# Softmax inverses taken through DRAM as 16 to a partition, and 21 weight-sum items placed in the first attention

## The chip, the cores and the metric

The kernel runs on one core of a Trainium2 chip. The metric is the device time of one execution in microseconds (us). Everything is computed in fp32.

## What is computed

Two layers, cut to what matters here:

```python
# layer 0: attention over the 1024 positions of each of 4 images, 1024 channels, 16 heads of 64
qkv = x @ w_qkv.T + b_qkv
q, k = rmsnorm(rope(q)), rmsnorm(rope(k))          # over all 1024 channels
attn = softmax(q @ k.T * 64 ** -0.5)
out = rmsnorm((attn @ v) @ w_proj.T) + x
# layer 1: 1x1 conv (1024 to 256), 3x3 conv (256 to 256), 1x1 conv (256 to 1024),
# each with batch norm over the 4 images; relu after the first two; then
x = relu(x + softplus(residual_scale) * out)
```

## The kernel before

**Stages.** The images go one after the other (`for b in range(B)`): the Q, K and V projections, attention, the output projection (called y). Then come the first 1x1 convolution, the 3x3 convolution and the last 1x1 convolution. Channels lie on the 128 partitions, in 8 tiles of 128 (NT); the 1024 positions of an image are the free axis, in two halves of 512 (NCH).

**Fast products.** The large products are done by a Strassen-Winograd scheme, one level in the first Q and K projections (`project`), two levels elsewhere (`project2`). It needs sums of weight blocks (S1 to S4) and sums of activations. Weight sums are made once and kept in DRAM for later images: the outer sums in `wd`, the inner ones in `wd2`. The function `operands` (L223) loads four blocks, makes four sums on VectorE (L231 to L234) for the product at hand and stores them to `wd` (L237). The other sums are "items": `prepare` (L382, sums L387 to L390, stores L392) and `prepare_blocks` (L395, sums L404 to L407, stores L409). An item is four loads of 256 KB, four VectorE operations and four stores of 256 KB. There are seven items for each of the four weights (WQ, WK, WV, WP), and four block items for WV and for WP.

**Who sets the order.** The order on every compute engine is written by hand; SyncE's (SP) order is set by a scheduler. Each queue runs in order, and an instruction that waits holds all that is behind it. In projections a pace is kept: `product_done` is called after each product (a product of the one-level scheme is one unit of pace, one of the two-level scheme half a unit), `after(n, step)` puts a step n units later, and `waiting` holds steps that are taken when there is room. `weight_parts(parts, first, step, lag, alloc)` starts an item's loads on GpSimd's queue (POOL) at `first + i * step` and makes its sums `lag` later.

**Attention.** `attention` (L740) runs once for each half of the queries (c), and within it over the 8 pairs of heads (hp). One such step is called a unit here, 16 to an image. A unit has 16 score products (L757) into three score banks, 8 exponentials on ScalarE (L764), 7 additions on VectorE that sum the exponentials into `den` (L766, L768), 16 steps of the product with V (L774), and a copy of the result into `q_all` (L779). After each odd unit, ones-products (`dn`, L800) turn the denominators of two units into a bank in which each 32 partitions hold one head's 512 denominators. At the start of the next unit `inverses` (L805) takes VectorE's reciprocal of the whole bank (L806) and sends one row per head to `dens` in DRAM, for a later check, and eight pieces from partition to partition into the tile `inv` (L814). At the end of the next odd unit `mean_of_v` multiplies the results by it (L737) and GpSimd adds a bias (L738).

At the end of a unit one step of `waiting` is taken (the last of K's rotation), and an `extra` step: the sums of the oldest item, and then at once the loads of another into the ring of eight weight buffers (`wring`); two items are in flight. In the first attention 15 items are done in this way, in the last one the sums of the 3x3 filters.

**The other places.** Of the remaining items, eight lie in the first Q projection (four blocks and four of WV), five in the first K projection (three of WV, two of WQ), three of WQ in the first V projection, two of WK in the first output projection, two in the second image's Q projection and one in its K projection. At the end of the image loop `conv1_first(1, ...)` (L899) does the first two products of the 1x1 convolution, and then `conv1_sums` (L873) makes the sums of its weights.

Of the kernel before, what the change touches and what calls it, by code (L numbers as in the profile page):

```python
# [18 lines left out]
P = 128  # L19
# [5 lines left out]
CH = 512  # L25
# [60 lines left out]
def program(ctx, tc, x, wblk, w2, w3, vecs, cos, sin, out, bad):  # L86
# [66 lines left out]
    with tc.tile_pool(name=f"st{u}", bufs=2) as st, ExitStack() as s:  # L153
# [70 lines left out]
        def operands(base, g, name):  # L224


            at = base // NT * NG + g
            a11, a12 = (block(base, g, ih, f"{name}_1{ih}") for ih in range(2))
            a21, a22 = (block(base, g + NG, ih, f"{name}_2{ih}") for ih in range(2))
            s1 = chunk(f"w_{name}_s1")  # L230
            nc.vector.tensor_tensor(s1, a21, a22, ALU.add)  # L231
            nc.vector.tensor_tensor(a21, a11, a21, ALU.subtract)
            nc.vector.tensor_tensor(a11, s1, a11, ALU.subtract)
            nc.vector.tensor_tensor(a12, a12, a11, ALU.subtract)  # L234
            spend(4 * TT)
            for o, t in enumerate((a11, s1, a21, a12)):
                nc.gpsimd.dma_start(wd[at, o], flat(t))  # L237
            return [a11, s1, a21, a12, a22]
# [501 lines left out]
        def attention(b, c, q_all, k_all, v, probs_, late, ready, extra, slow):  # L740
# [4 lines left out]
            for hp in range(NHP):  # L745
# [6 lines left out]
                for t in range(N // P):  # L752
                    p = probs_[:, t]
                    sc = bank("sc", f"sc_{n}_{t}")
                    for j in range(2):
                        d = slice(j * HD, (j + 1) * HD)
                        nc.tensor.matmul(  # L757
                            sc[:, j], k_all[d, hp, t * P : (t + 1) * P], q_all[d, hp, at],
                            start=True, stop=bad is not None,
                        )  # L760
                    if bad is None:
                        for j in range(2):
                            nc.tensor.matmul(sc[:, j], ones[0:1, :], rows[j], start=False, stop=True)
                    nc.scalar.activation(p, sc, AF.Exp)  # L764
                    if t == 1:
                        nc.vector.tensor_tensor(d_, probs[0], p, ALU.add)  # L766
                    elif t > 1:
                        nc.vector.tensor_tensor(d_, d_, p, ALU.add)  # L768
                    probs.append(p)
# [11 lines left out]
                if hp % 2 == 1:  # L781
                    for r in ready:
                        mean_of_v(q_all, *r)
                    ready.clear()
                if slow:
                    slow.pop(0)()

                left = (NCH - c) * NHP - hp - 1
                turn = bool(waiting)
                if turn:  # L790
                    next_waiting()
                if extra and (not turn or len(extra) >= left):
                    extra.pop(0)()
# [9 lines left out]

        def inverses(b, c, hp, n, dn, ready):
            r = temp(f"rec_{n}")  # L805
            nc.vector.reciprocal(r, dn)  # L806
            k = 2 * ((b * NCH + c) * NHP + hp - 1)
            if bad is not None:
                nc.sync.dma_start(dens[k : k + 4, :], r[::QH, :])
            w = big_temp(f"inv_{n}")  # L810
            for i in range(2):
                for j in range(4):
                    q = slice((2 * i + j // 2) * QH, (2 * i + j // 2 + 1) * QH)
                    nc.sync.dma_start(w[j * QH : (j + 1) * QH, half[i]], r[q, :])  # L814
                ready.append((c, hp - 1 + i, w[:, half[i]]))
# [249 lines left out]
        for b in range(B):  # L1065
# [12 lines left out]
            elif b == 1:  # L1078
                weight_parts([parts_of[WK][k] for k in (4, 5)], 8.5, 3.5, 3.5, pieces_of(room[:, : NT // 2, :]))
# [9 lines left out]
            elif b == 1:  # L1089
                weight_parts([parts_of[WK][6]], 11, 0, 3.5, pieces_of(room[:, : NT // 2, :]))  # L1090
# [3 lines left out]
            if b == 0:  # L1094
                two2 = [None, None, in_place(xs[b], ts[b], room, True)]

                t3 = pieces_of(xs[b][:, :NH, half[1]], 1)
                for k, at, free in ((6, 11, pieces_of(ts[b][1], 1)), (2, 14.5, t3), (3, 18.5, pieces_of(ts[b][1], 1))):
                    weight_parts([parts_of[WQ][k]], at, 0, 3.5, free)
# [6 lines left out]
            if b == 0:  # L1106
                todo = blocks_of(WP) + [parts_of[WP][k] for k in (0, 1, 6, 2, 3, 4, 5)]
                todo += [parts_of[WQ][k] for k in (4, 5)] + [parts_of[WK][k] for k in (0, 1)]
            made = []

            def extra_step():
                if len(made) == 2 or not todo:
                    made.pop(0)()
                if todo:
                    made.append(todo.pop(0)(pieces, nc.sync))

            extra = [extra_step] * len(todo)
            for _ in range(min(2, len(todo))):
                extra_step()
            if b == B - 1:  # L1120
                extra = filters()
            late, ready = [], []
# [9 lines left out]
            for c in range(NCH):  # L1132
                attention(b, c, q_all, k_all, v, probs_, late, ready, extra, slow)
# [45 lines left out]
            if b == 0:  # L1179
                weight_parts([parts_of[WK][k] for k in (2, 3)], 6, 7, 4, pieces_of(room[:, 3 * NT // 4 :, :]))  # L1180
# [14 lines left out]
        read_back(0)  # L1195
        conv1_first(1, back[1], w)
        ss = conv1_sums(w)
# [355 lines left out]
```

## Time and profile before

| | |
|---|---|
| Runs | 2701.3 us median of three, 2698.25 to 2702.26 |
| Profiled execution | 2699.65 us, of which its span is 2697.9 us |
| Instructions | 32539 |
| TensorE, VectorE, ScalarE, GpSimd busy | 98%, 81%, 41%, 17% |
| One attention unit on TensorE | 7.07 us of scores, 7.02 us of products with V; 1.0 us of dn after every second |
| Reciprocal of a 128x512 bank (L806) | 32 times, 3.354 us each |
| An addition of the denominators (L768) | 384 times, 1.225 us each |

The span is the stretch from the first to the last instruction of one profiled execution. A timeline lists the instructions of an engine in order of time, equal neighbours merged: its start, its duration, the line, the operation, the tile written and those read, how many, and in brackets how long the engine had been idle and which engine or transfer ended that. The busy times by stretch give, for each stretch of time, how long each engine was busy. Where TensorE is the engine without idle time, the idle time of the others costs nothing.

### The profile page before, as it was taken

The page shows a single profiled execution, that of the slowest core. Times are in us where ns is not written, and L with a number is a line of the kernel's source. Part 1 is how long each engine was busy: PE and PEld are TensorE (multiplying, and loading weights), DVE is VectorE, ACT ScalarE, POOL GpSimd, SP SyncE. Part 2 cuts the span into 40 slices and gives each one's busy share as a digit, 9 for nine tenths or more (in the row PEclk, how much of TensorE's full clock was granted, in tenths as well). Part 3 has the DMA queues.
Part 4 walks back from the last instruction along what each step waited for, and adds up shares of the span by engine and source line. Part 5 has one row for each costly group of instructions (what it writes and reads, how often), then busy time and mean ns, then how long its engine had stood idle before and what let it go on. Part 6 is the DMA issues. An engine that isn't in the chain of part 4 may idle for free. (4 is left out here: it accounts for less than half of the span.)

```text
span 2697.9 us, 32539 instructions
## 1 busy us (share of the span) xinstructions
PE 2656.7 (98%) x11386; PEld 1652.7 (61%) x11386; DVE 2194.8 (81%) x2529; ACT 1097.2 (41%) x1523; POOL 461.2 (17%) x568
## 2 busy tenths in 40 slices
PE   9999999999999999999999999999999999999997
PEld 4448433488888333688886333888884335846843
DVE  5577899998887977888878877887888878777987
ACT  2222455523342555333343555233525654312266
POOL 2562222222011211100111211100111211010000
PEclk9999999999999999999999999999999999999999
DMA  7897755587677341456765420665783323583165
GB/s 273 310 310 228 227 157 162 167 268 246 197 206 215 64 90 32 149 152 220 189 184 153 82 60 17 209 205 174 189 234 87 63 49 114 169 256 117 63 227 211
DMA packets 244811, 453.52 MB, mean 168 GB/s; under 512 B 28256, under 2 KB 117136, under 8 KB 244640
## 3 DMA queue, kind: packets, MB, share of 16 engines
q1 hardware_dynamic: 200112, 302.33, 35.7%
q0 software_dynamic: 44528, 149.02, 20.9%
q8 instruction: 93, 1.52, 0.2%
q14 instruction: 78, 0.64, 0.1%
HBM read 316.71 MB, written 96.78 MB: 153 GB/s over the span
## 5 line engine op out<-in xcount | busy, mean ns | idle before, releaser
L768 DVE TENSOR_TENSOR den<-den,p 128x1024 f32<-128x1024 f32 x384 | 470.5, 1225 | 40.7 <-DVE den L768 0.9
L764 ACT ACTIVATE p<-sc 128x1024 f32<-128x1024 f32 x512 | 476.3, 1043 | 54.9 <-PE sc L757 54.7
L757 PE MATMUL sc<-q,k 64*128 64x512 f32 x2048 | 457.7, 596 | 0.0
L757 PEld LDWEIGHTS sc<-q,k 64*128 64x128 f32 x2048 | 189.9, 186 | 265.5 <-issue 121.2
L774 PE MATMUL cx<-p,to 128*64 128x512 f32 x1536 | 340.2, 595 | 0.0
L774 PEld LDWEIGHTS cx<-p,to 128*64 128x64 f32 x1536 | 106.0, 137 | 228.2 <-issue 228.2
L738 POOL TENSOR_SCALAR q<-q,vec 128x512 f32<-128x512 f32 x64 | 123.7, 1939 | 561.7 <-DVE q L737 561.7
L458 PE MATMUL p_y<-q,w_y 128*128 128x256 f32 x928 | 210.1, 380 | 1.1 <-DMA w_y<-wdf 1.1
L453 PE MATMUL p_v<-w_v,x 128*128 128x256 f32 x928 | 210.1, 380 | 0.6 <-DVE x L424 0.6
L458 PEld LDWEIGHTS p_y<-q,w_y 128*128 128x128 f32 x928 | 175.9, 190 | 28.5 <-issue 4.8
L453 PEld LDWEIGHTS p_v<-w_v,x 128*128 128x128 f32 x928 | 176.5, 190 | 25.8 <-DVE x L424 1.3
L779 ACT COPY q<-cx 128x512 f32<-128x512 f32 x64 | 37.6, 587 | 356.9 <-PE cx L774 356.9
L458 PE MATMUL p_k<-to,w_k 128*128 128x256 f32 x672 | 153.1, 381 | 4.7 <-ACT to L547 4.7
L458 PE MATMUL p_q<-to,w_q 128*128 128x256 f32 x672 | 152.5, 380 | 0.7 <-ACT q L512 0.6
L458 PEld LDWEIGHTS p_k<-to,w_k 128*128 128x128 f32 x672 | 126.7, 190 | 25.8 <-ACT to L547 7.1
L458 PEld LDWEIGHTS p_q<-to,w_q 128*128 128x128 f32 x672 | 127.2, 190 | 20.2 <-ACT q L512 1.9
L766 DVE TENSOR_TENSOR den<-p 128x1024 f32<-128x1024 f32 x64 | 76.5, 1195 | 76.2 <-ACT p L764 76.2
L806 DVE RECIPROCAL rec<-dn 128x512 f32<-128x512 f32 x32 | 107.3, 3352 | 20.6 <-PE dn L800 20.6
L774 PE MATMUL cx<-p,rq 128*64 128x512 f32 x512 | 113.4, 595 | 0.0
L1457 PE MATMUL c<-h,w 128*128 128x512 f32 x256 | 110.3, 592 | 0.9 <-ACT h L1359 0.9
L700 POOL DMA_DIRECT2D k<-ks x64 | 55.6, 1011 | 276.5 <-ACT p L764 110.9
L453 PE MATMUL p_v<-w_v,t 128*128 128x256 f32 x384 | 91.6, 384 | 3.6 <-DMA w_v<-in_wblk_dram 3.6
(479 smaller groups left out, 4212.8 us busy)
## 6 DMA issues: line engine op xcount, KB each, us to landing
w_v<-wd2f SPq DMA_DIRECT2D x112, 256.0 KB
w_y<-wd2f SPq DMA_DIRECT2D x112, 256.0 KB
w_q<-wd2f SPq DMA_DIRECT2D x84, 256.0 KB
w_k<-wd2f SPq DMA_DIRECT2D x84, 256.0 KB
x<-in_x_dram SPq DMA_DIRECT2D x64, 256.0 KB
q<-qs POOLq DMA_DIRECT2D x64, 256.0 KB, 5.6
k<-ks POOLq DMA_DIRECT2D x64, 256.0 KB, 4.6
inv<-rec SPq DMA_DIRECT2D x256, 64.0 KB
```

The costliest lines, as they stand in the source:

```text
L453: nc.tensor.matmul(o[:, q].rearrange("p (g f) -> p g f", g=2), r[:, i, q * P : (q + 1) * P], wt[:, :, i, :], skip_group_check=True, **at,)
L458: nc.tensor.matmul(o[:, q], wt[:, q, i, :], r[:, i, :], skip_group_check=True, **at)
L700: nc.gpsimd.dma_start(dst[i::2, f, :], other[1 - i :: 2, :], accum_op=ALU.add)
L738: nc.gpsimd.tensor_scalar(cx, cx, col("bv", hp), None, ALU.add)
L757: nc.tensor.matmul(sc[:, j], k_all[d, hp, t * P : (t + 1) * P], q_all[d, hp, at], start=True, stop=bad is not None,)
L764: nc.scalar.activation(p, sc, AF.Exp)
L766: nc.vector.tensor_tensor(d_, probs[0], p, ALU.add)
L768: nc.vector.tensor_tensor(d_, d_, p, ALU.add)
L774: nc.tensor.matmul(o[j * HD : (j + 1) * HD, :], v[:, t, h0 : h0 + HD], probs[t][:, j], start=(t == 0), stop=(t == N // P - 1),)
L779: nc.scalar.copy(q_all[:, hp, at], o)
L806: nc.vector.reciprocal(r, dn)
L1457: nc.tensor.matmul(os[i], w3t[k][f // NH][:, f % NH, :], h2[b, k][:, half[c]], start=(k == 0), stop=(k == NPT - 1),)
```

## The change

Five edits:

- `operands` stores its four sums from ScalarE's queue instead of GpSimd's, one product later.
- In attention the denominators of four heads are copied by ScalarE, written to DRAM as rows, and read back as 16 to a partition; at the end of the next (even) unit VectorE inverts this 128x16 tile in place, it is written back to the same rows, and eight broadcasts from DRAM fill `inv`. The last pair of units of an image keeps the old way.
- 21 items instead of 15 are done in the first attention: six come from other places (one of WQ from the first V projection, five of WK from the first output projection and the second image's Q and K projections), and the two WQ items that stay in the first V projection are timed anew. They are spread evenly over 15 units, so that units 2, 4, 7, 9, 12 and 14 (counted from 0) make two. The last attention's filter sums are spread by the same rule.
- The loads of an item begin after the fourth score block of a unit (`t == 3`) rather than at the end of the unit before.
- `conv1_sums` is called ahead of `conv1_first`.

```diff
@@ -233,8 +233,12 @@
             nc.vector.tensor_tensor(a11, s1, a11, ALU.subtract)
             nc.vector.tensor_tensor(a12, a12, a11, ALU.subtract)
             spend(4 * TT)
-            for o, t in enumerate((a11, s1, a21, a12)):
-                nc.gpsimd.dma_start(wd[at, o], flat(t))
+
+            def keep():
+                for o, t in enumerate((a11, s1, a21, a12)):
+                    nc.scalar.dma_start(wd[at, o], flat(t))
+
+            after(1, keep)
             return [a11, s1, a21, a12, a22]
 
 
@@ -737,7 +741,7 @@
             nc.vector.tensor_tensor(cx, cx, w, ALU.mult)
             nc.gpsimd.tensor_scalar(cx, cx, col("bv", hp), None, ALU.add)
 
-        def attention(b, c, q_all, k_all, v, probs_, late, ready, extra, slow):
+        def attention(b, c, q_all, k_all, v, probs_, late, ready, extra, slow, steps_in_all, load_parts):
 
 
             at = half[c]
@@ -762,6 +766,8 @@
                         for j in range(2):
                             nc.tensor.matmul(sc[:, j], ones[0:1, :], rows[j], start=False, stop=True)
                     nc.scalar.activation(p, sc, AF.Exp)
+                    if t == 3:
+                        load_parts()
                     if t == 1:
                         nc.vector.tensor_tensor(d_, probs[0], p, ALU.add)
                     elif t > 1:
@@ -782,14 +788,15 @@
                     for r in ready:
                         mean_of_v(q_all, *r)
                     ready.clear()
+                if half_done:
+                    half_done.pop(0)()
                 if slow:
                     slow.pop(0)()
 
-                left = (NCH - c) * NHP - hp - 1
-                turn = bool(waiting)
-                if turn:
+                if waiting:
                     next_waiting()
-                if extra and (not turn or len(extra) >= left):
+                slots = NCH * NHP - 1
+                for _ in range(len(extra) - -(-steps_in_all * max(slots - 1 - c * NHP - hp, 0) // slots)):
                     extra.pop(0)()
                 if hp % 2 == 0:
                     continue
@@ -801,17 +808,36 @@
                 sums_ = []
                 late.append(lambda *a, n=n, hp=hp, dn=dn: inverses(b, c, hp, n, dn, ready))
 
+        half_done = []
+
         def inverses(b, c, hp, n, dn, ready):
+
+
             r = temp(f"rec_{n}")
-            nc.vector.reciprocal(r, dn)
             k = 2 * ((b * NCH + c) * NHP + hp - 1)
-            if bad is not None:
+            if (c, hp) == (NCH - 1, NHP - 1):
+                nc.vector.reciprocal(r, dn)
                 nc.sync.dma_start(dens[k : k + 4, :], r[::QH, :])
+                spread(c, hp, n, ready, [r[q * QH : (q + 1) * QH, :] for q in range(4)])
+                return
+            nc.scalar.copy(r, dn)
+            nc.sync.dma_start(dens[k : k + 4, :], r[::QH, :])
+            few = st.tile([P, 4 * CH // P], F32, tag="few", name=f"few_{n}")
+            rows = dens[k : k + 4, :].rearrange("r (a t) -> (r a) t", t=4 * CH // P)
+            nc.sync.dma_start(few, rows)
+
+            def invert():
+                nc.vector.reciprocal(few, few)
+                nc.sync.dma_start(rows, few)
+                spread(c, hp, n, ready, [dens[k + q, :].partition_broadcast(QH) for q in range(4)])
+
+            half_done.append(invert)
+
+        def spread(c, hp, n, ready, rows):
             w = big_temp(f"inv_{n}")
             for i in range(2):
                 for j in range(4):
-                    q = slice((2 * i + j // 2) * QH, (2 * i + j // 2 + 1) * QH)
-                    nc.sync.dma_start(w[j * QH : (j + 1) * QH, half[i]], r[q, :])
+                    nc.sync.dma_start(w[j * QH : (j + 1) * QH, half[i]], rows[2 * i + j // 2])
                 ready.append((c, hp - 1 + i, w[:, half[i]]))
 
         def o_norm(b, total, ys):
@@ -1075,8 +1101,6 @@
                 unused = kp.tile([P, NT, N], F32, tag="k", name="unused")
                 parts = blocks_of(WV) + [parts_of[WV][k] for k in (0, 1, 6, 2)]
                 weight_parts(parts, 8, 2.4, 4, pieces_of(unused))
-            elif b == 1:
-                weight_parts([parts_of[WK][k] for k in (4, 5)], 8.5, 3.5, 3.5, pieces_of(room[:, : NT // 2, :]))
             tq = qk_proj(b, WQ, xs[b], ts[b], "bq", q_all, "q", w1 if b == 0 else None, two, True)
             rope(b, q_all, tq, eps_q, HD / C, None, "q", b == 0)
             k_all = kp.tile([P, NT, N], F32, tag="k", name=f"k_{b}")
@@ -1086,17 +1110,13 @@
             if b == 0:
                 parts = [parts_of[WV][k] for k in (3, 4, 5)] + [parts_of[WQ][k] for k in (0, 1)]
                 weight_parts(parts, 2, 4.5, 4, pieces_of(room))
-            elif b == 1:
-                weight_parts([parts_of[WK][6]], 11, 0, 3.5, pieces_of(room[:, : NT // 2, :]))
             tk = qk_proj(b, WK, xs[b], ts[b], "bk", k_all, "k", None, two)
             rope(b, k_all, tk, eps_rms, 1.0 / C, (wqk_other, wqk), "k")
             v = room
             if b == 0:
                 two2 = [None, None, in_place(xs[b], ts[b], room, True)]
 
-                t3 = pieces_of(xs[b][:, :NH, half[1]], 1)
-                for k, at, free in ((6, 11, pieces_of(ts[b][1], 1)), (2, 14.5, t3), (3, 18.5, pieces_of(ts[b][1], 1))):
-                    weight_parts([parts_of[WQ][k]], at, 0, 3.5, free)
+                weight_parts([parts_of[WQ][k] for k in (6, 2)], 11.5, 6.5, 4, pieces_of(ts[b][1], 1))
             project2(b, 1, WV, *two2[2], b == 0, v, True, "v", lambda c: None)
 
             rest(leave=4 if b > 0 else 2)
@@ -1105,21 +1125,19 @@
             todo = []
             if b == 0:
                 todo = blocks_of(WP) + [parts_of[WP][k] for k in (0, 1, 6, 2, 3, 4, 5)]
-                todo += [parts_of[WQ][k] for k in (4, 5)] + [parts_of[WK][k] for k in (0, 1)]
+                todo += [parts_of[WQ][k] for k in (3, 4, 5)] + [parts_of[WK][k] for k in (0, 1, 6, 2, 3, 4, 5)]
             made = []
 
-            def extra_step():
-                if len(made) == 2 or not todo:
-                    made.pop(0)()
-                if todo:
+            def load_parts():
+
+                while todo and len(made) < 2:
                     made.append(todo.pop(0)(pieces, nc.sync))
 
-            extra = [extra_step] * len(todo)
-            for _ in range(min(2, len(todo))):
-                extra_step()
+            extra = [lambda: made.pop(0)()] * len(todo)
+            load_parts()
             if b == B - 1:
                 extra = filters()
-            late, ready = [], []
+            late, ready, steps_in_all = [], [], len(extra)
 
             def add_residual(f, b=b - 1):
                 nc.gpsimd.dma_start(
@@ -1130,7 +1148,7 @@
             slow = [lambda: None] * 3 + [lambda f=f: add_residual(f) for f in range(NT)] if b > 0 else []
             probs_ = xp.tile([P, N // P, 2, CH], F32, tag="x", name=f"p_{b}")
             for c in range(NCH):
-                attention(b, c, q_all, k_all, v, probs_, late, ready, extra, slow)
+                attention(b, c, q_all, k_all, v, probs_, late, ready, extra, slow, steps_in_all, load_parts)
             psum_for("proj")
             room = v_room(f"to_{b}")
             tc_ = [
@@ -1176,8 +1194,6 @@
 
                 for i in range(0, NH, 2):
                     after(14 + 3 * i, lambda i=i: waiting.append((5 * TT, lambda: first_sums(i))))
-            if b == 0:
-                weight_parts([parts_of[WK][k] for k in (2, 3)], 6, 7, 4, pieces_of(room[:, 3 * NT // 4 :, :]))
             yt[b] = kp.tile([P, NT, N], F32, tag="k", name=f"y_{b}")
             two = (2, *in_place(q_all, tc_, yt[b], False), True)
             if b + 1 < B:
@@ -1193,8 +1209,8 @@
         read_back(2)
         back[0] = v_room("back")
         read_back(0)
+        ss = conv1_sums(w)
         conv1_first(1, back[1], w)
-        ss = conv1_sums(w)
         for i in range(0, NH, 2):
             t_sums(back[1], None, t2[i], i, range(3, 4))
         room1, sums2 = t1, t2
```

## The prediction

> **What bounds the kernel now.** I read the page's busy times first, then TensorE's timeline from end to end for its gaps, then the same stretches on VectorE (DVE), ScalarE (ACT), GpSimd (POOL) and SyncE's queue (SP), then the busy times by stretch. The first line of the page:
>
> ```profile
> PE 2656.7 (98%) x11386; PEld 1652.7 (61%) x11386; DVE 2194.8 (81%) x2529; ACT 1097.2 (41%) x1523; POOL 461.2 (17%) x568
> ```
>
> TensorE is idle for 2697.9 - 2656.7 = 41.2 us. Its timeline puts 5.75 of that ahead of the first matmul and 15.1 behind the last one (which ends at 2669.76 + 13.04 = 2682.8). About 20 us lie between, and no edit here changes the matmuls, so only these can be won. The larger gaps, from TensorE's timeline (start, us, then in brackets the idle time before it and who ended it):
>
> ```profile
> 168.23 3.70 PE L298 MATMUL pa_k<-t,w_k_2b 128*128 128x512 f32 x8 [0.94 <-DVE w_k_2b L233]
> 187.30 3.70 PE L298 MATMUL pa_k<-t,w_k_3b 128*128 128x512 f32 x8 [1.63 <-DVE w_k_3b L233]
> 276.81 3.40 PE L453 MATMUL p_v<-w_v,t 128*128 128x256 f32 x8 [3.65 <-DMA w_v<-in_wblk_dram]
> 280.01 2.21 PE L453 MATMUL p_v<-w_v,x 128*128 128x256 f32 x8
> 282.06 1.89 PE L453 MATMUL p_v<-w_v,t 128*128 128x256 f32 x8
> ...
> 563.53 1.97 PE L458 MATMUL p_y<-q,w_y 128*128 128x256 f32 x8 [1.10 <-DMA w_y<-wdf]
> 662.80 1.99 PE L458 MATMUL p_q<-t,w_q 128*128 128x256 f32 x8 [0.67 <-DMA w_q<-wdf]
> 749.35 1.99 PE L458 MATMUL p_k<-t,w_k 128*128 128x256 f32 x8 [0.56 <-DMA w_k<-wdf]
> 783.05 7.17 PE L458 MATMUL p_k<-to,w_k 128*128 128x256 f32 x32 [2.35 <-ACT to L547]
> 1359.42 7.17 PE L458 MATMUL p_k<-to,w_k 128*128 128x256 f32 x32 [0.81 <-ACT to L547]
> 2362.05 5.37 PE L894 MATMUL c<-t,c_S 128*128 128x512 f32 x8 [3.06 <-DVE c_S L878]
> 2367.26 3.60 PE L894 MATMUL c1s<-to,c_S 128*128 128x512 f32 x8
> ```
>
> Two gaps cost more than they show. After 3.65 us the next eight matmuls take 280.01 - 276.81 = 3.20 us from start to start and the next 2.05, against 1.73 elsewhere: 1.47 + 0.32 more, 5.44 in all. After 3.06 us they take 5.21 against 3.43: 1.78 more, 4.84 in all. After 2.35 us nothing is lost.
>
> The four attentions, by stretch (PE, PEld, DVE, ACT, POOL busy; clock; DMA share; GB/s):
>
> ```profile
> 295.96:530.69 234.73, 234.66 (x1089) 84.08 (x1088) 220.99 (x203) 129.83 (x145) 66.20 (x82) 1.00 0.54 164
> 879.00:1113.00 234.00, 234.00 (x1092) 84.50 (x1090) 186.19 (x150) 129.71 (x145) 40.97 (x36) 1.00 0.27 55
> ```
>
> TensorE has no gap there: the first attention, with DVE 94% busy, is 0.7 us longer than the second. A faster DVE in attention buys nothing. The question is where the moved work stops hurting, and whether the fuller first attention stays covered.
>
> **What the Trainium skill says.** "TensorE: Matmul & The Clock Gate", Part 1, says that an idle window of about 3.4 us, which is free-running, drops the array to half clock. This trace agrees: near half rate after 3.65 and 3.06 us, none after 2.35. "DMA: Bandwidth & Descriptors", section Issuing engines are not separate DMA queues, says that DMAs of ACT, SP and POOL share 16 engines and another issuer saves only issue time. So I expect ACT's stores to relieve POOL's queue, not the bandwidth. Anatomy of one DMA, same page, puts a small DMA at about 2 us, mostly completion; here the 4 KB inv_df write of L676 lands after 2.1 us.
>
> **The change, part by part.**
>
> *Sums of the last convolution's weights (conv1_sums) ahead of conv1_first.* DVE is idle from 2354.3 to 2359.1, waiting for TensorE's c1a (L910), and the four sums queue behind that. Moved ahead, they run in the idle time (4 x about 0.68 = 2.7 us) and are ready near 2357; TensorE wants them at 2358.99. Of their ring slots the last is freed when p_y ends at 2352. The gap and its clock loss go: 4.84. Next late is the sum of squares for ss_y: its DVE adds (L588) and one ACT square end about 0.5 us after TensorE would now arrive. Gain 4.3.
>
> *Third weight item in the first V projection goes to attention; the others start at 11.5 and 18.* Between 260 and 280 us the DMA share is 1.03 at 334 GB/s. The load that TensorE misses was issued at 266.3 and was needed at 273.2, among an item's load on POOL (258 to 261.5, landing 9.5 us after issue), another's stores (260.9 to 265.4) and a rope accumulation. The item of 258 goes away: 1 MB of loads and 1 MB of stores. What is left is one item's stores ahead and the next load behind. Between 0 and 5.44 gained; I take 4.0.
>
> *Operand stores of the first Q and K from POOL to ACT.* Each set takes POOL 4 x 0.54 us, 3.6 with its waits at 168.6. Behind it stand the item loads that DVE then waits for (5.37 us ahead of 182.32), and DVE's lateness makes the 0.94 and 1.63 gaps. On ACT the four issues (SP's take 0.36 each, so about 1.5 us) wait for the DVE sums; behind them ACT has squares and the copy of the A22 product. The next copy that TensorE needs is a product later (3.43 us) or more, so this is covered unless the sums come over 3 us late, when TensorE waits for them anyway. But the DMA share is 1.02 here and stays. 0 to 2.6 gained; I take 2.0.
>
> *Items out of the first output projection (two), second Q (two) and second K (one).* Each is 2.9 us of DVE, 1 MB in and 1 MB out, on POOL. Loads sit just ahead of the gaps: 547.8 before 563.53, 660.7 before 662.80, 741.9 before 749.35; the 783.05 gap is 0.81 in later images, which have no items. Winnable: 1.10 + 0.67 + 0.56 + (2.35 - 0.81) + a 0.63 gap at 621.38 behind a busy DVE = 4.5. I take 3.5.
>
> *Softmax inverses.* 28 of 32 reciprocals (3.354 us) go: 94 us of DVE, hidden, worth nothing by themselves. Added: an ACT copy (0.59, like L779's) behind dn while the first scores run (0.9 us), so covered; and a 128x16 reciprocal, which the trace doesn't show: the 128x256 row is 1.75 and 128x512 3.35, so a line through them gives 0.24 us; bounds 0.1 and 1. The chain is now denominators to DRAM, back as 128x16, inverted at the end of the next unit, to DRAM, eight broadcasts back. On SP the eight take 5 to 6 us, with 2 us each side: about 10 us from a reciprocal to its multiplication L737, which DVE reaches 12 to 15 us later.
>
> *21 items instead of 15 in the first attention.* Let E be the start of an even unit; a unit is 14.09 us. From DVE's timeline, denominators start at the earliest 3.15 us into a unit and end at 12.36:
>
> ```profile
> 402.10 1.22 DVE L766 TENSOR_TENSOR den<-p 128x1024 f32<-128x1024 f32 x1 [0.22 <-ACT p L764]
> 403.43 7.88 DVE L768 TENSOR_TENSOR den<-den,p 128x1024 f32<-128x1024 f32 x6
> 411.22 1.29 DVE L737 TENSOR_TENSOR q<-q,inv 128x512 f32<-128x512 f32 x2
> ```
>
> The spread rule makes two items in units 2, 4, 7, 9, 12 and 14. For an even one: 12.36 + 0.3 + 2 x 2.9 = E + 18.5, the odd unit's denominators take 9.2 more, E + 27.7; TensorE needs them for dn at E + 28.2. It fits by 0.5 us. The small read must land by E + 12.4. On SP it stands behind weight loads that wait for POOL's stores of the unit before, which stand behind POOL's two 2.1 us bias adds: stores from E + 3.1, first landing (2.8) near E + 6.2, read landing about E + 11 to 12. So near nothing, with little room: between 0.7 gained (the first attention's excess) and some 10 lost. I take 1.5 lost. In the later attentions DVE has 48 of 234 us free: nothing.
>
> Sum: 4.3 + 4.0 + 2.0 + 3.5 - 1.5 = 12.3. The profiled execution took 2699.65 (span 2697.9, 1.75 around it), so 2687.35. The median of the runs shown is 2701.3, 1.65 above it: 2689.0.
>
> **The rivals.** (A) Bandwidth, not POOL's order, makes the K and V gaps, and they stay (for it: shares of 1.02 and 1.03; against: 2 MB leave the V stretch). 4.3 + 3.5 - 1.5 = 6.3 gained: 2695.0. (B) The small reads land 3 us later than I think, the double units' reciprocals wait, and dn waits 2.5 us in four pairs: 13.8 - 10 = 3.8 gained, 2697.5. For it: SP's order, and the 0.5 us of room; against: landings of 2.3 to 4.6 us in this stretch. (C) Slower: the broadcasts from DRAM land after L737 wants them, and DVE stands with everything behind it. In the first attention a pair has 3.6 us of slack there, so TensorE loses what exceeds that, seven times; in the others the slack is near 9.9 us. At 7 us late: 7 x 3.4 = 24 lost, 13.8 - 24 = 10 worse, 2711. It decides from 6.3 us late. For it: three dependent DMAs where one was, all on SP's queue; against: 2.1 us for a small write, 0.6 per broadcast issue.
>
> **How the numbers follow.** My forecast 0.52, A 0.18, B 0.17, C 0.13. About 0.2% (5.4 us) is what measurement can tell from no change. Faster by more: forecast and A, 0.70; within: B, 0.17; slower: C, 0.13. The best ends give 4.8 + 5.4 + 2.6 + 4.5 + 0.7 = 18, 2683.3; with the runs' spread, 2682. Upward the range takes in A and B, to 2699, and leaves out C.
>
> **What would show it.** The gap at c_S gone; no wait for w_v near 273; gaps at w_k_2b and w_k_3b under 0.5; 783's gap at 0.8; the first attention within 234.0 to 236.5. Waits of DVE before the 128x16 reciprocal or L737 with gaps at dn would make it B or C; unchanged K and V gaps, A.

## The result, and the profile after

The changed kernel takes 2690.1 us (median of 7 runs, 2688.6 to 2694.9), the kernel before 2701.3 (median of 7 runs, 2698.3 to 2707.1). The ratio is 0.9959, with a 95% interval of 0.9948 to 0.9971: about 11 us faster, against 12.3 in the forecast (2689.0). The profiled execution of the changed kernel took 2691.15 us, its span 2689.1, so the two profiled executions are only 8.5 us apart: before's was 1.65 under its median, this one is 1.0 over its own. What follows from single profiles is read against these 8.5.

The first line of the page after:

```profile
PE 2655.3 (99%) x11386; PEld 1650.9 (61%) x11386; DVE 2109.6 (78%) x2529; ACT 1112.6 (41%) x1551; POOL 426.8 (16%) x512
```

VectorE has lost 85 us of work and TensorE 1.4. The gain is not the 85; it is idle time of TensorE that went, 41.2 us before and 2689.1 - 2655.3 = 33.8 now, and clock losses. TensorE's timeline after, at the places that were shown of before:

```profile
9.27 15.14 PE L302 MATMUL pa_q<-x,w_q 128*128 128x512 f32 x30 [1.54 <-DMA x<-in_x_dram]
...
189.39 5.40 PE L302 MATMUL pa_k<-t,w_k_3b 128*128 128x512 f32 x8 [2.54 <-DVE w_k_3b L233]
...
256.97 1.97 PE L457 MATMUL p_v<-w_v,t 128*128 128x256 f32 x8 [0.73 <-DMA w_v<-wdf]
...
777.50 7.17 PE L462 MATMUL p_k<-to,w_k 128*128 128x256 f32 x32 [0.81 <-ACT to L551]
...
2354.97 3.60 PE L920 MATMUL c<-t,c_S 128*128 128x512 f32 x8
2358.41 3.60 PE L920 MATMUL c1s<-to,c_S 128*128 128x512 f32 x8
2362.04 0.64 PE L670 MATMUL ss_y<-sqy,ones 128*32 128x256 f32 x8
```

The gap ahead of c_S is gone and so is its clock loss; the 3.65 ahead of w_v has become 0.73 at another place; 2.35 has become 0.81. But the gap ahead of w_k_3b, the last of K0's four sets of operands, has grown, with a clock loss of its own, and the first line is new: a wait for x at the start of the kernel.

To see what every edit does, I take the time at which TensorE starts each stage, and from it each stage's length. This table carries most of what follows; each number is from one profile (us). "Q0" is the first image's Q projection, "C1" the first 1x1 convolution.

| Stage | before | after | difference |
|---|---|---|---|
| Q0 | 98.81 | 101.28 | +2.47 |
| K0 | 100.01 | 101.40 | +1.39 |
| V0 | 91.40 | 86.76 | -4.64 |
| first attention | 234.73 | 234.54 | -0.19 |
| Y0, Q1, K1 | 263.34 | 258.82 | -4.52 |
| C1 | 105.33 | 100.44 | -4.89 |
| all the others, and the start | | | +1.65 |
| end of the last matmul | 2682.80 | 2674.07 | -8.73 |

How far one profile carries can be read from two kernels below whose code is that of the kernel before up to the end of V0 (sums first alone, inverses alone). There K0 is 101.44 and 101.99 us, against 100.01 in the table, and V0 88.83 and 89.15, against 91.40. So in these two stages a difference of up to 2.6 us can come without any edit. Y0, Q1 and K1 together repeat better: 263.3 to 264.5 us in the four kernels with the old items there, 258.1 to 260.2 in the nine without.

The attentions, by stretch (the columns are as in the prediction):

```profile
295.12:529.66 234.54, 234.47 (x1089) 84.41 (x1088) 214.46 (x226) 133.80 (x152) 77.47 (x106) 1.00 0.68 218
873.95:1107.39 233.44, 233.44 (x1090) 84.28 (x1089) 163.77 (x149) 133.79 (x152) 42.27 (x36) 1.00 0.28 55
```

With six items more, the first attention has less VectorE work than before (214.5 against 221.0 us) and is no longer.

### The profile page after: what moved, and what is told of

Its sections match the earlier page's. It is cut to its first block, busy times and chain, and to the rows that moved or that the text cites. A ratio compares the mean times of both kernels' runs of the same rounds, so it can differ in the third digit from the quotient of the medians.

```text
span 2689.1 us, 32699 instructions
## 1 busy us (share of the span) xinstructions
PE 2655.3 (99%) x11386; PEld 1650.9 (61%) x11386; DVE 2109.6 (78%) x2529; ACT 1112.6 (41%) x1551; POOL 426.8 (16%) x512
## 5 line engine op out<-in xcount | busy, mean ns | idle before, releaser
L462 PE MATMUL p_y<-to,w_y 128*128 128x256 f32 x384 | 90.4, 380 | 0.9 <-DMA w_y<-wdf 0.8
```

What stands on the lines that cost most here:

```text
L462: nc.tensor.matmul(o[:, q], wt[:, q, i, :], r[:, i, :], skip_group_check=True, **at)
```

## The experiments

All kernels here compute the whole reference. The stage lengths are again from one profile of each.

**One part alone: sums first, ACT stores, inverses.** Three kernels, each the kernel before with one edit.

```diff
+        ss = conv1_sums(w)
         conv1_first(1, back[1], w)
-        ss = conv1_sums(w)
```

> The kernel before with one edit: conv1_sums ahead of conv1_first. My theory: the gap of 3.06 us at c_S and its clock loss of 1.78 us go, some 0 to 0.5 us comes back at ss_y: 4.3 to 4.9 us faster than before, and every stage up to the last output projection as in the kernel before. Rival (the gap is only moved to the next wait, for back or for ss_y): under 1.5 us faster, with a new gap within 20 us behind the old one.

Measured: 2695.2 us against 2701.4, ratio 0.9979 (0.9972 to 0.9986). C1 goes from 105.33 to 100.44, the same as in the changed kernel. That the stages ahead would be as before did not hold: K0 is 1.4 us longer and V0 2.6 shorter, with nothing edited there. In the changed kernel the sums stand well ahead of their use, and the squares for ss_y end at 2358.91 + 3.07 = 2361.98, just as TensorE comes for them at 2362.04:

```profile
2349.74 0.69 DVE L903 TENSOR_TENSOR c_S<-w_c_last,w_c_last 128x512 f32<-128x512 f32 x1
...
2358.91 3.07 DVE L592 TENSOR_TENSOR sqy<-sqy,sq_y 128x512 f32<-128x512 f32 x4
```

So the whole 4.89 is won; the 0.5 that I had taken off for ss_y isn't lost.

```diff
-            for o, t in enumerate((a11, s1, a21, a12)):
-                nc.gpsimd.dma_start(wd[at, o], flat(t))
+            def keep():
+                for o, t in enumerate((a11, s1, a21, a12)):
+                    nc.scalar.dma_start(wd[at, o], flat(t))
+
+            after(1, keep)
```

> The kernel before with one edit: the operand stores of the first Q and K on ScalarE's queue, one product later. If POOL's queue made the gaps in K (as I took it in the prediction): 2 us faster, both gaps of K under 0.5 us. If bandwidth makes them (rival A): within 1 us of before, or some us slower; one gap of K stays, its wait ended by a load of the weights[...].

Measured: 2705.0 us, ratio 1.0010 (1.0003 to 1.0018). The edit costs some 3 us where I had forecast a gain of 2. TensorE's timeline of this kernel:

```profile
9.67 16.13 PE L302 MATMUL pa_q<-x,w_q 128*128 128x512 f32 x30 [1.89 <-DMA x<-in_x_dram]
...
189.56 3.70 PE L302 MATMUL pa_k<-t,w_k_3b 128*128 128x512 f32 x8 [1.44 <-DVE w_k_3b L233]
```

The gap at w_k_3b stays (1.63 before), and the new wait for x is there: Q0 is 102.30, 3.5 us longer than before. This gave a new theory, which the trace of POOL's queue suggests. In the kernel before, POOL stands for 30 us with the first store, and the item loads stand behind it:

```profile
32.41 0.57 POOL L237 DMA_DIRECT2D wdf<-w_q_0b  x1 [30.44 <-DVE w_q_0b L233]
...
34.56 2.14 POOL L401 DMA_DIRECT2D unused<-in_wblk_dram  x4
```

In the changed kernel nothing holds POOL, and eight item loads (2 MB, of which the first sums are stored only at 52.45 us) are issued at once:

```profile
1.95 3.74 POOL L405 DMA_DIRECT2D unused<-in_wblk_dram  x7
7.36 0.54 POOL L405 DMA_DIRECT2D unused<-in_wblk_dram  x1 [1.67 <-DMA vec<-in_vecs_dram]
```

They meet the loads of x and w_q. SyncE's queue, first before and then after, shows these taking up to twice as long to issue:

```profile
3.06 1.60 SPq L221 DMA_DIRECT2D w_q<-in_wblk_dram  x3
4.70 2.87 SPq L210 DMA_DIRECT2D x<-in_x_dram  x4
```

```profile
3.07 3.15 SPq L221 DMA_DIRECT2D w_q<-in_wblk_dram  x3
6.26 4.28 SPq L210 DMA_DIRECT2D x<-in_x_dram  x4
```

The activation sums on VectorE that start at 17.14 us before start at 23.84 after, waiting for x, and everything behind them is late. The runs on the stores below put this to the test.

The third kernel has the new `inverses`, `spread` and `half_done` and nothing else.

```diff
-            nc.vector.reciprocal(r, dn)
...
+            nc.scalar.copy(r, dn)
+            nc.sync.dma_start(dens[k : k + 4, :], r[::QH, :])
+            few = st.tile([P, 4 * CH // P], F32, tag="few", name=f"few_{n}")
+            rows = dens[k : k + 4, :].rearrange("r (a t) -> (r a) t", t=4 * CH // P)
+            nc.sync.dma_start(few, rows)
...
+                nc.vector.reciprocal(few, few)
```

> The kernel before with the softmax inverses through DRAM as 16 to a partition, and nothing else; 15 items in the first attention as before. My theory: 94 us of VectorE saved off the critical path, so within 1 us of before; all attentions 233.4 to 234.8 us long. Rival (the longer chain through DRAM holds VectorE): slower by 5 us or more, gaps at dn or at the scores, and waits of over 3 us before L737.

Measured: 2701.4 us, ratio 1.0000 (0.9991 to 1.0008). Taking 94 us of reciprocals off VectorE is worth nothing by itself, and the chain of three transfers costs nothing.

**The items without the inverses.** The changed kernel with the old reciprocal for every pair.

```diff
-            if (c, hp) == (NCH - 1, NHP - 1):
+            if True:
```

> The changed kernel with the old inverses for all pairs: the reciprocal of the whole bank on VectorE, 21 items in the first attention. My theory: the inverses' only worth is VectorE's room for the items; here a pair of units needs 18.2 (denominators) + 3.35 + 1.3 + 21/8 x 2.9 (items) + 0.7 (slower beside GpSimd) = 31.2 us of VectorE against 29.17 of TensorE, so the first attention gets 8 to 14 us longer and the kernel as much slower than the changed one (within 4 us of the kernel before, either side). Rival (room was there anyway, spreading is enough): within 1.5 us of the changed kernel.

Measured: 2703.9 us, ratio to before 1.0012 (1.0004 to 1.0020), so 14 us above the changed kernel. The first attention is 247.17 us, 12.6 longer. VectorE waits for nothing in that stretch, and dn waits for VectorE; VectorE's and TensorE's timelines of this kernel:

```profile
375.15 7.87 DVE L774 TENSOR_TENSOR den<-den,p 128x1024 f32<-128x1024 f32 x6
...
387.59 3.34 DVE L819 RECIPROCAL rec<-dn 128x512 f32<-128x512 f32 x1
```

```profile
380.60 1.05 PE L807 MATMUL dn<-den,ones 128*32 128x512 f32 x4
383.08 1.05 PE L807 MATMUL dn<-den,ones 128*32 128x512 f32 x4 [1.43 <-DVE den L774]
```

The gap that is printed is less than what is lost: normally the eight dn matmuls take 1.0 us together, here it is 383.08 + 1.05 - 380.60 = 3.5. So the inverses are what makes room for 21 items.

**Where the stores stand.** First the changed kernel with all operand stores back on POOL, then with only the first set there.

```diff
-            def keep():
-                for o, t in enumerate((a11, s1, a21, a12)):
-                    nc.scalar.dma_start(wd[at, o], flat(t))
-
-            after(1, keep)
+            for o, t in enumerate((a11, s1, a21, a12)):
+                nc.gpsimd.dma_start(wd[at, o], flat(t))
```

> The changed kernel with the operand stores of the first projections back on POOL at once; the three other parts stay. Theory (POOL's wait for the first sums had held the eight item loads back until about 32 us, and without it they issue at 1.95 us and compete with x and w_q): Q0 returns from 101.3 to 98 or 99 us, first matmuls as before; K0 stays between 98.8 and 102 because its gaps come from late w_k loads; V0 near 87 to 89. Time 1 to 3 us below the changed kernel, 2687 to 2689. Rival (the prediction's own term: ACT stores close K gaps worth 2.0): K0 2 us longer than in the changed kernel and Q0 unchanged, 2692.

Measured: 2687.7 us, ratio to before 0.9946 (0.9931 to 0.9960). Q0 98.96, K0 99.60.

```diff
+            first = name.startswith("q_0_0")
+
             def keep():
                 for o, t in enumerate((a11, s1, a21, a12)):
-                    nc.scalar.dma_start(wd[at, o], flat(t))
+                    (nc.gpsimd if first else nc.scalar).dma_start(wd[at, o], flat(t))
 
-            after(1, keep)
+            if first:
+                keep()
+            else:
+                after(1, keep)
```

> The changed kernel with only the first operand set of Q0 stored from POOL at once, the others from ACT a product later. This keeps the eight item loads behind the wait for w_q_0b and changes nothing else. Theory (early item loads are what lengthened Q0): POOL's item loads start at about 34 us and not at 1.95, Q0 returns to 98 to 99 us, the time is 2 to 3.5 us below the changed kernel, 2686.5 to 2688.5. Rival (the stores' place on ACT, its 0.33 us an issue or the waits there, lengthened Q0): Q0 stays at 101 to 102, time unchanged at 2690.

Measured: 2687.3 us, ratio to before 0.9939 (0.9924 to 0.9954). Q0 97.78, K0 98.93. POOL's and TensorE's timelines of this kernel:

```profile
31.80 0.57 POOL L241 DMA_DIRECT2D wdf<-w_q_0b  x1 [29.84 <-DVE w_q_0b L233]
...
33.95 3.74 POOL L410 DMA_DIRECT2D unused<-in_wblk_dram  x7
```

```profile
5.73 15.55 PE L307 MATMUL pa_q<-x,w_q 128*128 128x512 f32 x32 [5.73 <-DMA x<-in_x_dram]
```

The item loads start at 33.95 us again, the wait for x is gone, and Q0 is as short as ever, with 12 of 16 stores of Q0 and all of K0 on ScalarE. So it is the early loads and not the place of these 12 stores. Nor is it the place of the first set: in the changed kernel TensorE is already 2.3 us behind (its first product with w_q_0b starts at 38.22 us, against 35.90 before) when ScalarE issues the first of its stores, at 38.15. The intervals of these two and of the changed kernel overlap; the total alone would not settle 3 us, but the stage does: in all eight kernels of this study in which the first set is stored from POOL, Q0 is 97.8 to 99.2 us, and in the five in which it isn't, 101.0 to 102.3.

The length of K0 doesn't tell where its sums are stored from: 99.6 to 102.0 us in the four kernels that store them from POOL, 98.8 to 101.6 in the six that store them from ScalarE with the same items around. But its waits do. VectorE's timeline before, and then after:

```profile
182.32 0.69 DVE L387 TENSOR_TENSOR rq<-rq 128x512 f32<-128x512 f32 x1 [5.37 <-DMA rq<-in_wblk_dram]
...
185.11 0.68 DVE L231 TENSOR_TENSOR w_k_3b_s<-w_k_3b,w_k_3b 128x512 f32<-128x512 f32 x1
```

```profile
182.12 0.69 DVE L391 TENSOR_TENSOR rq<-rq 128x512 f32<-128x512 f32 x1 [2.88 <-DMA rq<-in_wblk_dram]
...
187.19 0.69 DVE L231 TENSOR_TENSOR w_k_3b_s<-w_k_3b,w_k_3b 128x512 f32<-128x512 f32 x1 [2.21 <-DMA w_k_3b<-in_wblk_dram]
```

With the stores on POOL (four kernels), VectorE waits 5.2 to 6.1 us for the load of a WQ item, and the sums of w_k_3b then follow without a wait; TensorE has a gap ahead of w_k_2b (0.31 to 0.94 us) and one ahead of w_k_3b. With them on ScalarE and that item in place (seven kernels), the wait for the item is 2.2 to 3.4 us and the gap at w_k_2b is gone, but VectorE then waits 1.3 to 2.2 us for w_k_3b itself. So POOL's queue did hold the item's load back (issued from 172.26 us before, from 168.08 after), and releasing it only let the next wait end last: 0.94 and 1.63 us of gaps before, 2.54 in one piece after.

**The third item in the first V projection.** The changed kernel with that item back there, at the old times.

```diff
-                weight_parts([parts_of[WQ][k] for k in (6, 2)], 11.5, 6.5, 4, pieces_of(ts[b][1], 1))
+                t3 = pieces_of(xs[b][:, :NH, half[1]], 1)
+                for k, at, free in ((6, 11, pieces_of(ts[b][1], 1)), (2, 14.5, t3), (3, 18.5, pieces_of(ts[b][1], 1))):
+                    weight_parts([parts_of[WQ][k]], at, 0, 3.5, free)
...
-                todo += [parts_of[WQ][k] for k in (3, 4, 5)] + [parts_of[WK][k] for k in (0, 1, 6, 2, 3, 4, 5)]
+                todo += [parts_of[WQ][k] for k in (4, 5)] + [parts_of[WK][k] for k in (0, 1, 6, 2, 3, 4, 5)]
```

> The changed kernel with the third WQ item back in V0 at the old times, 20 items in the first attention. Theory (three single items close on each other in V0 made w_v late): V0 goes from 86.8 back to 88.5 to 91.5 with a gap of 2.8 or more ahead of the w_v matmuls near 273 us, the first attention unchanged at 234.5 (its DVE has room either way); time 2 to 5 us above the changed kernel, 2692 to 2695. Rival (bandwidth, not the items, made w_v late, and V0's gain came with the stores' queue): V0 stays at 86.8, time unchanged at 2690.

Measured: 2694.7 us, 4.5 above the changed kernel; ratio to before 0.9973 (0.9964 to 0.9983). V0 is 89.35, 2.6 longer, and the gap is back, in TensorE's timeline:

```profile
280.67 2.00 PE L457 MATMUL p_v<-w_v,t 128*128 128x256 f32 x8 [2.60 <-DMA w_v<-in_wblk_dram]
```

This run puts back the third item and the old times of the two others together; which of them makes the gap was not separated.

**The loads in the middle of a unit.** The changed kernel with an item's loads begun after the unit's end.

```diff
-                    if t == 3:
-                        load_parts()
...
                     extra.pop(0)()
+                    load_parts()
```

> The changed kernel with the item loads of the first attention begun after the unit's end as in the kernel before, not in its middle. Theory (the place of the loads hides either way, as a load of 2 to 5 us has a unit of 7 to 16 us of room): first attention 234.4 to 235.0, time within 1.5 us of the changed kernel. Rival (the loads at the unit's end would meet the small transfers of the inverse or come too late for the sums): gaps at dn or at the Y0 projection's w_y matmuls, first attention 236 or more, time 2 to 6 us longer.

Measured: 2696.7 us, ratio to before 0.9982 (0.9974 to 0.9989), 6.6 above the changed kernel. My theory, that the place of the loads is hidden, fell. The first attention is 240.01 us, 5.5 longer. TensorE's timeline shows one of two such places (the other, with 1.68 us, is at 471.89):

```profile
438.12 1.05 PE L806 MATMUL dn<-den,ones 128*32 128x512 f32 x4
440.01 1.05 PE L806 MATMUL dn<-den,ones 128*32 128x512 f32 x4 [0.84 <-DVE den L772]
```

The denominators were late because VectorE had stood for the small read ahead of the 128x16 reciprocal:

```profile
427.86 0.25 DVE L829 RECIPROCAL few<-few 128x16 f32<-128x16 f32 x1 [4.11 <-DMA few<-densf]
```

And the read was late because of SyncE's queue, here in this kernel and then in the changed one, around the same pair:

```profile
415.02 0.51 SPq L823 DMA_DIRECT2D densf<-rec  x1
415.62 8.32 SPq L382 DMA_DIRECT2D w_pre<-wdf  x7
423.99 0.46 SPq L826 DMA_DIRECT2D few<-densf  x1
```

```profile
418.05 0.51 SPq L824 DMA_DIRECT2D densf<-rec  x1
418.65 3.22 SPq L382 DMA_DIRECT2D w_pre<-wdf  x3
422.93 0.43 SPq L827 DMA_DIRECT2D few<-densf  x1
423.46 3.45 SPq L382 DMA_DIRECT2D w_pre<-wdf  x4
```

With the loads at the unit's end seven of them stand between the write of the denominators and their read back, 8.3 us; begun in the middle, three do, and the others come behind the read. The stretch starts 3 us earlier in the first kernel (its scores start at 424.03, those of the changed one at 427.09), so against the unit the read is issued 4.1 us later.

**What is left at w_k_3b.** With the gap at w_k_3b open in every kernel so far, one WQ item more was moved from K0 to attention (22 items), on top of the kernel with the first set on POOL.

```diff
-                parts = [parts_of[WV][k] for k in (3, 4, 5)] + [parts_of[WQ][k] for k in (0, 1)]
+                parts = [parts_of[WV][k] for k in (3, 4, 5)] + [parts_of[WQ][k] for k in (0,)]
...
-                todo += [parts_of[WQ][k] for k in (3, 4, 5)] + [parts_of[WK][k] for k in (0, 1, 6, 2, 3, 4, 5)]
+                todo += [parts_of[WQ][k] for k in (1, 3, 4, 5)] + [parts_of[WK][k] for k in (0, 1, 6, 2, 3, 4, 5)]
```

> The kernel with the first operand set on POOL, and one WQ item more moved from the first K projection to the first attention, which then makes 22. Theory (transfers, not the place of the stores, make w_k_3b late: 2 MB less in a stretch with a DMA share of 1.04 close the gap): no gap ahead of the w_k_3b matmuls, K0 goes from 98.9 to 97.1 or 97.5. In attention a 22nd item makes a seventh double unit; a double even unit has 0.5 to 1.0 us of room ahead of dn, a double odd unit more, so the stage stays between 234.5 and 236. Time 2685 to 2687. Rival (K's gap comes from DVE standing for an item's load ahead of the w_k_3b sums, whichever item it is, and attention has no room for 22): the gap stays at 1.4 or more, attention 237 or more, 2689 to 2692.

Measured: 2689.8 us, ratio to before 0.9952 (0.9938 to 0.9966). K0 98.84, the gap 1.68; attention 237.04. The run doesn't decide on the gap: the item taken out was the last one, whose transfers come behind w_k_3b. TensorE's timeline, and VectorE's with what stands ahead:

```profile
186.37 3.70 PE L307 MATMUL pa_k<-t,w_k_3b 128*128 128x512 f32 x8 [1.68 <-DVE w_k_3b L233]
```

```profile
179.74 0.69 DVE L396 TENSOR_TENSOR rq<-rq 128x512 f32<-128x512 f32 x1 [2.72 <-DMA rq<-in_wblk_dram]
184.17 0.69 DVE L231 TENSOR_TENSOR w_k_3b_s<-w_k_3b,w_k_3b 128x512 f32<-128x512 f32 x1 [1.55 <-DMA w_k_3b<-in_wblk_dram]
```

First a wait for an item's load, then, after its four sums, one for w_k_3b itself. Attention with 22 items is 2.5 us longer here than with 21, and 1.0 in the next kernel (235.50). That kernel puts the WQ item that is left in K0 behind w_k_3b, in the same 22-item kernel:

```diff
-                weight_parts(parts, 2, 4.5, 4, pieces_of(room))
+                free = pieces_of(room)
+                weight_parts(parts[:3], 2, 4.5, 4, free)
+                weight_parts(parts[3:], 20, 0, 4, free)
```

> The 22-item kernel of the run before, with the WQ item that stays in the first K projection begun at unit 20 of pace and not at 15.5, so that its loads and stores come behind the loads of w_k_3b (the run before had only taken the item that came behind them anyway). Theory (transfers and the wait for this item's load on VectorE make w_k_3b late): no gap ahead of w_k_3b, K0 from 98.8 to 97.1 or 97.4, no wait of VectorE ahead of the w_k_3b sums. Rival (w_k_3b is late for another cause, such as the buffer it is loaded into coming free late): the gap stays at 1.4 or more. Time near the run before, 2689, less up to 2.

Measured: 2685.2 us, ratio to before 0.9950 (0.9933 to 0.9967). K0 is 96.90 and the gap is gone, in TensorE's timeline. VectorE's still shows a wait for w_k_3b, but 4.4 us earlier and hidden:

```profile
184.10 3.60 PE L307 MATMUL pa_k<-t,w_k_3b 128*128 128x512 f32 x8
```

```profile
179.78 0.69 DVE L231 TENSOR_TENSOR w_k_3b_s<-w_k_3b,w_k_3b 128x512 f32<-128x512 f32 x1 [3.13 <-DMA w_k_3b<-in_wblk_dram]
```

So this item, by its transfers ahead of w_k_3b and by its sums ahead of the operand sums, made the gap. No run separates the two. In the run before this one VectorE had finished the item's sums and then waited 1.55 us more for w_k_3b, nearly the whole gap of 1.68; so where the stores are on ScalarE, the late load is the larger part.

The last kernel does the same with 21 items, both WQ items of K0 late (`weight_parts(parts[3:], 20, 2, 4, free)`).

> The kernel with the first operand set on POOL and 21 items in attention, with both WQ items of the first K projection begun late, at units 20 and 22 of pace instead of 15.5 and 20. Theory (the item ahead of w_k_3b makes the gap, and attention at 21 items costs nothing): K0 96.9 to 97.3, attention 234.5, V0 86.6 to 88 as the second item's stores now reach into it; 2683 to 2686. Rival (the moved item only carries the conflict into the V projection): V0 89 or more with a gap at a w_v matmul, 2687 or more.

Measured: 2689.2 us, ratio to before 0.9954 (0.9936 to 0.9972). K0 96.90 and attention 234.55 as in the theory, but V0 is 88.78, with a new gap in TensorE's timeline, whose releaser the profile doesn't name:

```profile
207.34 3.69 PE L462 MATMUL p_v<-w_v,rq 128*128 128x256 f32 x16 [1.94 <-issue]
```

Presumably the conflict that left K0 partly came back in V0; the profile doesn't show it. The kernel before, run beside each of the last three, had medians of 2702.0, 2699.2 and 2703.3 us, so these three are compared by their ratios, which don't tell them apart. The changed kernel has five variants here that store the first set from POOL. Their ratios to before are the lowest of all (0.9939 to 0.9954), but their intervals overlap with the changed kernel's 0.9948 to 0.9971.

## Why the prediction came out right, and the step that failed

The time came within 1.1 us of the forecast, and part of that is luck. By the two profiles one term had the wrong sign and missed by 5.9 us, later stages lost 1.65, and the four other terms together gained 3.9 more than I had taken.

- *Sums first: 4.3.* Right; 4.89. The squares for ss_y are in time.
- *Third item out of V0: 4.0 of 0 to 5.44.* Right in kind; 4.64 in the profile of after, and putting it back costs 4.5 by the medians, 2.6 by the profile of V0. The size swings: with before's items in V0, the stage is 88.8, 89.2, 89.4, 91.4 and 93.5 us in the five kernels that have them; with the third item out it is 85.8 to 87.3 in seven of eight (88.8 in the last kernel above). So the two groups are 1.5 us apart at their closest, and what a single profile shows above that depends on the execution. The DMA share hardly fell (from 257 to 277 us 1.02 at 287 GB/s after, 1.04 at 318 before); that the item's transfers stood ahead of the w_v load is argued from the traces, and the new times of the other two may have a part.
- *Operand stores on ScalarE: 2.0 of 0 to 2.6.* **This step failed.** Measured alone it costs about 3 us, and in the changed kernel Q0 is 2.5 longer. I had written that item loads stand behind the stores on POOL, and took their release for a gain in K0. I didn't ask what the same release does at the start, where the store's wait of 30.44 us was what kept eight loads away from x and w_q. The lower end of the range for this term, zero, had no reason behind it. In K0 the release happened as forecast (VectorE's wait for the item fell from 5.37 to 2.88 us, the gap at w_k_2b went), but I had not asked which wait would end last then: it was the load of w_k_3b, and the two gaps became one of 2.54 that cost clock as well. Only taking the item from ahead of w_k_3b closed it. A late load at a DMA share of 1.03 (150 to 205 us) fits rival A for K0; for V0, where the gap went at 1.02, A is wrong.
- *Items out of Y0, Q1 and K1: 3.5 of 4.5.* Right, and all of it came: 0.37 + 1.78 + 2.37 = 4.52. That the 783.05 gap would shrink to the 0.81 of later images came out to the digit.
- *Inverses: nothing, and 1.5 lost in the first attention.* Nothing, and nothing lost. (The excess of 0.7 us of the first attention over the second that I had read was too small, since my stretch for the second began 0.5 us ahead of its first score product; it is 1.3, and 0.19 of it went.) The 128x16 reciprocal takes 0.25 us; the line through 128x256 and 128x512 had given 0.24. The working for a double even unit is confirmed step by step. With E = 354.67 (the start of its scores) VectorE's timeline of after has:

```profile
366.94 0.24 DVE L830 RECIPROCAL few<-few 128x16 f32<-128x16 f32 x1
...
372.61 1.22 DVE L772 TENSOR_TENSOR den<-p 128x1024 f32<-128x1024 f32 x1
373.93 7.88 DVE L774 TENSOR_TENSOR den<-den,p 128x1024 f32<-128x1024 f32 x6
381.72 1.29 DVE L741 TENSOR_TENSOR q<-q,inv 128x512 f32<-128x512 f32 x2
```

  The denominators of the even unit end at E + 12.3 (12.36 in the working), the two items at E + 17.9 (18.5), those of the odd one at E + 27.05 (27.7), and dn starts at 382.84, E + 28.17 (28.2): 1.1 us of room where I had 0.5. VectorE does wait for the small read, but so little that the room takes it up. Where it waited, the read took 3.0 to 5.2 us from its issue, where my working had 2. The two longest waits fell in even units with one item, which have more room; the double ones waited 0.6 us at most. The waits in the first attention (total, times, longest):

```profile
DVE few L830 <- DMA few<-densf: 4.2, 5, 1.4
```

- *Rivals.* B's mechanism exists: it is what happens when the loads are begun at the unit's end (waits of 4.1 us, gaps at dn, 6.6 us lost). In the changed kernel the fourth edit keeps it away. The prediction has no term for that edit, and ahead of the experiment I took it for worth nothing. C didn't come: no wait ahead of the multiplication by `inv` in any attention.

The sum again, as the two profiles have it: 4.89 + 4.64 - 3.86 (Q0 and K0) + 4.52 + 0.19 = 10.38, less 1.65 elsewhere, is 8.73. The 1.65 is spread over later stages, about half of it, 0.85, in the last output projection; its cause stays open. From 8.5 to the medians' 11.2 it is 2.7, which is where the two profiled executions lie against their medians (1.65 under, 1.0 over). K0 is one place where single executions differ: 101.40 in this profile of after and 101.59 in one more kernel with the same stores and items in K0, 98.8 to 98.9 in three others.

## What to carry to other kernels

A wait in an in-order queue also holds back what stands behind it; before moving it, list the first instructions that come free, when they will now be issued, and whom they meet. A faster engine off the path is worth what is put in its place: the inverses alone gave nothing, everything else without them was 2.5 us slower than before, and together they freed the other stages. When one wait is shortened, look for the one that will then end last. Don't let a small transfer that is waited for stand behind a whole batch of large ones on its queue: behind seven, the small read was issued 4.1 us later in its unit than behind three.

## What the runs showed of the hardware that was not expected

*A gap of 2 us can cost clock.* The Trainium skill, "TensorE: Matmul & The Clock Gate", Part 1, has a free-running window of about 3.4 us, and I took gaps under 3 us for free, since 2.35 had cost nothing. In the kernel with the inverses alone, two gaps of that size cost 1.7 and 1.6 us more; its timeline, and the busy times over the first of the two, with the granted clock (0.67) behind POOL's column:

```profile
186.98 5.40 PE L298 MATMUL pa_k<-t,w_k_3b 128*128 128x512 f32 x8 [2.37 <-DVE w_k_3b L233]
...
781.09 8.78 PE L458 MATMUL p_k<-to,w_k 128*128 128x256 f32 x32 [2.34 <-ACT to L547]
```

```profile
186.98:192.22 5.24, 5.24 (x9) 2.25 (x10) 2.53 (x4) 1.26 (x2) 2.37 (x5) 0.67 1.04 386
```

Eight matmuls take 5.40 us instead of 3.70, and the 32 take 8.78 (at a clock of 0.81) instead of 7.17 (at 1.00) after the same gap in the kernel before. Over the kernels, gaps ahead of w_k_3b of 2.00, 2.37, 2.54 and 2.73 us cost this, and those of 1.34 to 1.76 didn't. A gap of 2.34 or 2.35 in the second image's K projection cost it in two kernels and did not in two. Gaps of 2.60, 2.77 and 2.95 ahead of w_v cost nothing. So these runs give no length from which on a gap costs, only that 2.00 us can be enough, well below 3.4. That the same gap costs in one execution and not in another fits a window that runs on its own clock, but no run here shows the window.

*The issuing engine.* That DMAs of several engines share the same 16 DMA engines ("DMA: Bandwidth & Descriptors", Issuing engines are not separate DMA queues) shows here as a price: three w_q issues on SyncE took 3.15 us instead of 1.60 while POOL's loads were under way.
